# A graph network's first stage: statistics, keys, checks and attention vectors made ahead of the loop over node blocks

## The chip, the core and the metric

The kernel runs on one core of a Trainium2 chip. A core has TensorE (PE, matrix products, with its weight loads shown as PEld), VectorE (DVE), ScalarE (ACT), GpSimd (POOL) and SyncE (SP), which issues most DMA transfers. The engines run side by side, each through its own list of instructions in order, and wait for each other by semaphores. The metric is the device time of one execution in microseconds (us); lower is better.

## The reference

The reference takes 3125 nodes with 256 features and 100,000 directed edges, sorted by target, and computes four residual blocks one after the other:

```python
x = x + gat2(layernorm(x))        # two graph attention layers: 4 heads of 256, then 1 head of 256
x = x + experts8(layernorm(x))    # the two best of 8 experts, chosen for all nodes together
x = x + gcn3(layernorm(x))        # linear, then two graph convolutions, each with relu
x = x + experts8_per_node(layernorm(x))   # two of 8 experts per node
```

Of the attention layer, this is what the changed stage prepares:

```python
h    = (x @ W1).reshape(N, 4, 256)
al_s = einsum('nhc,hc->nh', h, a_src)     # source logit of each node and head
al_d = einsum('nhc,hc->nh', h, a_dst)     # target logit
e    = leaky_relu(al_s[src] + al_d[dst], 0.2)
out  = segment_sum(h[src] * softmax_over_incoming(e), dst)
```

## The kernel before, in words

The nodes are 25 blocks of 128, held in five groups of five blocks. The logits need no `h`: W1 times the attention vectors gives one matrix `u1` of 256 x 8, and the normalised features times `u1` give all eight logits of a node. Likewise `u2` serves the second layer from W2.

The function concerned is `FirstLayer.run` (line 2080 on). Its first part, in the pool named `before`, does the following.

- `bounds` (L1418 on) finds first and last target of each chunk of 256 edges. `load_edges` loads sources and targets.
- `norm_rows` (L1538 on) normalises a group in two halves: statistics on VectorE (L1544, L1545), then a root on ScalarE (L1548), reciprocal and product on VectorE (L1549, L1550), five normalisations on ScalarE (L1553) and a store of the rows into a DRAM table (L1555).
- `attention_vectors` (L1570) makes `u1` or `u2`: 16 VectorE instructions of 128x256, each a product with its sum.
- `count_starts` (L1452 on), `keys` (L1505 on), `edge_starts` (L1462 on) and `check` (L1479 on) are VectorE work on the edge lists: where each chunk writes, the keys by which edges are counted, and flags that say whether the fast way was allowed.
- The loop over 25 blocks turns each block on TensorE (L2127, two transposes into PSUM, two PSUM buffers), copies it to `xt` on ScalarE (L2131), stores five blocks at a time to DRAM (L2133) and multiplies it with `u1` into the logits `pl` (L2135). At every fourth block a `count_step` goes along: it makes one-hot matrices of a chunk of edges on VectorE (L1666, L1669), multiplies them on TensorE (L1683) and adds the counts to `acc` on ScalarE and VectorE (L1700, L1705). The one-hot matrices have three buffers.
- `sd` takes the logits out of PSUM (L2137). `first_terms` reduces them to their extremes, over the partitions on GpSimd (L1589), and after its first `yield` makes the terms of the attention weights (L1596 on). SP writes them to the DRAM table behind the rows (L1598), to `terms` (L1602) and to `loops` (L1612). Six count steps stand between the two halves.

After that the pool `before` is closed, and its room goes to the buffers of the main loop (`open_sums`). GpSimd begins to gather source rows from the table (L1790), one indirect DMA per 128 edges, eight to a batch, with room for three batches. SP loads turned blocks and the self-loops' weights, broadcast to all partitions (L1914, L1916), and for each chunk a window of target terms and the places of its edges (L1800, L1803). VectorE joins gathered terms with target terms (L1833) and spreads the weights over the one-hot matrices (L1844). TensorE sums the gathered rows by target (L1856), and VectorE adds the sums up (L1873). The main loop interleaves these edge steps with the count steps and with a dense part for the 256 lowest targets.

What sets the order: VectorE's instructions of the first part are tied to the written order (`k.in_order` with VectorE alone). TensorE, ScalarE, GpSimd and the queues of the first part are ordered by the framework's scheduler. In the main loop the written order holds for TensorE, VectorE and ScalarE. A tile takes the room of a closed pool only when all users of that room are done.

In the part that changes, the order of the source before is this:

```python
for g in range(GR + 1):            # statistics and normalisation of five groups
    ...
    if g == 2:
        self.attention_vectors("1", tmp, u1, ...)
self.count_starts(tmp); self.keys(tmp)
for b in range(NB): ...            # turn, copy, store, multiply; xt has two buffers
```

Of the kernel before, what the change touches and what calls it, by code (L numbers as in the profile page):

```python
# [11 lines left out]
F32 = mybir.dt.float32  # L12
# [12 lines left out]
P = 128  # L25
# [3 lines left out]
D = 256  # L29
# [1361 lines left out]
class FirstLayer:  # L1391
# [692 lines left out]
    def run(self, src_cols, dst_cols, dst_rows, x_in, keep, stats, u2):  # L2084

        tc, nc, k, I = self.tc, self.nc, self.k, self.I
        with ExitStack() as ctx:
            pool = ctx.enter_context(tc.tile_pool(name="edges", bufs=1))
            self.open_counts(ctx, pool)
            w1 = pool.tile([P, 2, 4 * D], F32, name="w1_all")  # L2090
            with tc.tile_pool(name="before", bufs=1) as tmp, \
                    tc.tile_pool(name="ps_in", bufs=1, space=PSUM) as psum, \
                    tc.tile_pool(name="ps_turn", bufs=2, space=PSUM) as turn:
                start = len(nc.cur_bb.bb.instructions)
                self.bounds(dst_rows, tmp)
                self.load_edges(src_cols, dst_cols, tmp)
                nc.gpsimd.dma_start(w1, I["L0_gnn_W1"].rearrange("(c p) f -> p c f", p=P))
                for b in range(0, NB, GB):
                    last_x = nc.sync.dma_start(
                        k.x[:, b:b + GB, :],  # L2100
                        x_in[b * P:(b + GB) * P, :].rearrange("(b p) f -> p b f", p=P))
                nc.vector.memset(k.rows[:, :, D:], 1.0)
                groups = [self.norm_rows(
                    k.x[:, b:b + GB, :],
                    self.table[b * P:(b + GB) * P, :D].rearrange("(b p) f -> p b f", p=P), tmp)
                    for b in range(0, NB, GB)]
                u1 = tmp.tile([P, 2, 8], F32, name="u1")
                for g in range(GR + 1):
                    if g < GR:
                        next(groups[g])  # L2110
                    if g == 2:
                        self.attention_vectors("1", tmp, u1,
                                               w1.rearrange("p c (k f) -> p k c f", k=4))
                    if g > 0:
                        next(groups[g - 1])
                self.count_starts(tmp)
                self.keys(tmp)
                pl = psum.tile([P, 512], F32, name="pl")
                sd = tmp.tile([P, NB, 8], F32, name="sd")
                i = 0  # L2120
                for b in range(NB):
                    if b % 4 == 0:
                        self.count_step(i)
                        i += 1
                    pt = turn.tile([P, 512], F32, name="turn")
                    for c in range(2):
                        nc.tensor.transpose(pt[:, ts(c, P)], k.x[:, b, ts(c, P)], k.ident)  # L2127
                    if b % GB == 0:
                        xt5 = tmp.tile([P, 2, GW], F32, name="xt", bufs=2)
                    xt = xt5[:, :, ts(b % GB, P)]  # L2130
                    nc.scalar.copy(xt, pt[:, :2 * P].rearrange("p (c n) -> p c n", c=2))  # L2131
                    if b % GB == GB - 1:
                        nc.sync.dma_start(self.turned[:, :, (b + 1) * P - GW:(b + 1) * P], xt5)  # L2133
                    for c in range(2):
                        nc.tensor.matmul(pl[:, 8 * b:8 * b + 8], lhsT=xt[:, c, :],  # L2135
                                         rhs=u1[:, c, :], start=(c == 0), stop=(c == 1))
                nc.vector.tensor_copy(sd.rearrange("p b k -> p (b k)"), pl[:, :8 * NB])  # L2137
                w2 = tmp.tile([P, 8, D], F32, name="w2")
                load = nc.gpsimd.dma_start(w2, I["L0_gnn_W2"].rearrange("(c p) f -> p c f", p=P))
                tc.add_manual_dep(load.ins, last_x.ins.name, SYNC)  # L2140
                parts = self.first_terms(sd, pool)
                next(parts)
                self.edge_starts(tmp)
                for _ in range(6):
                    self.count_step(i)
                    i += 1
                next(parts)
                self.attention_vectors("2", tmp, u2, w2.rearrange("p (k c) f -> p k c f", c=2))
                self.check(tmp)
                k.in_order({}, start, [mybir.EngineType.DVE])  # L2150
            self.open_sums(ctx, w1, stats)
            for c in range(RB * BC):
                self.fetch(c)
            for task in self.new_sums(0):
                task()
                self.count_step(i)
                i += 1
            self.tasks.extend(self.new_sums(1))
            for m in range(2):
                for c in range(self.size[m]):  # L2160
                    self.window(m, c)
            self.count_step(i)
            i += 1
            self.place_edges(0)
            self.pick_terms(0)
            self.count_step(i)
            i += 1
            self.place_edges(1)
            self.weigh_edges(0)
            self.spread_edges(0)  # L2170
            self.open_dense()
            e = s = 0
            i0, d0 = i, CUT[1] + 6
            engines, last = [mybir.EngineType.PE, mybir.EngineType.DVE, mybir.EngineType.Activation], {}
            start = len(nc.cur_bb.bb.instructions)

            d1 = d0 + 3
            while i < C1 + 3 or e <= NE or s < len(self.steps) or self.tasks or self.later:
                if i < C1 + 3:
                    self.count_step(i)  # L2180
                if i == d0:
                    self.lead(0)
                later, self.later = self.later, []
                if self.tasks:
                    self.tasks.popleft()()
                share = (FIRST * (i - i0) / (d1 - i0) if i < d1 else
                         FIRST + (NE + 1 - FIRST) * (i - d1) / (C1 - d1))
                while e <= NE and e <= share:
                    self.edge_step(e)
                    if e == NE:  # L2190
                        self.tasks.extend(self.through_w1(AS - 1))
                    e += 1
                while s < len(self.steps) and i > d0 + 3 and \
                        s * (C1 - 12 - d0) <= (i - d0 - 3) * len(self.steps):
                    self.dense_step(s)
                    s += 1
                for f in later:
                    f()
                start = k.in_order(last, start, engines)
                i += 1  # L2200
# [490 lines left out]
```

## Time and profile before

| | us |
|---|---|
| median of 4 runs | 2582.72 |
| the runs | 2575.94, 2579.74, 2585.70, 2598.34 |
| the profiled execution's own time | 2580.89 |
| its span | 2579.1 |
| TensorE busy | 2289.0 (89%) |
| VectorE busy | 1379.2 (53%) |
| ScalarE busy | 1152.6 (45%) |
| GpSimd busy | 828.6 (32%) |
| mean granted TensorE clock | 0.932 |
| first gather issued | 103.91 |

Busy time is the sum of an engine's instructions. In the rows of the timeline the columns are: start in us from the span's start, length in us, engine, line of the source, operation, what it writes and reads, and in brackets how long the engine had been idle and what ended that. A releaser in brackets is inferred from semaphores: where an instruction waits for several, it is the one that came last. An engine name with a q (SPq, POOLq) is that engine's sequencer, where DMA transfers are issued.

### The profile page before, as it was taken

The page shows a single profiled execution, that of the slowest core. Times are in us where ns is not written, and L with a number is a line of the kernel's source. Part 1 is how long each engine was busy: PE and PEld are TensorE (multiplying, and loading weights), DVE is VectorE, ACT ScalarE, POOL GpSimd, SP SyncE. Part 2 cuts the span into 40 slices and gives each one's busy share as a digit, 9 for nine tenths or more (in the row PEclk, how much of TensorE's full clock was granted, in tenths as well). Part 3 has the DMA queues.
Part 4 walks back from the last instruction along what each step waited for, and adds up shares of the span by engine and source line. Part 5 has one row for each costly group of instructions (what it writes and reads, how often), then busy time and mean ns, then how long its engine had stood idle before and what let it go on. Part 6 is the DMA issues. An engine that isn't in the chain of part 4 may idle for free. (4 is left out here: it accounts for less than half of the span.)

```text
span 2579.1 us, 38754 instructions
## 1 busy us (share of the span) xinstructions
PE 2289.0 (89%) x11821; PEld 1866.6 (72%) x11821; DVE 1379.2 (53%) x4362; ACT 1152.6 (45%) x2556; POOL 828.6 (32%) x803
## 2 busy tenths in 40 slices
PE   2489989998989987779999699979989989999996
PEld 2378777877767664668888588858867667888886
DVE  6677666677777874217888623433326663111110
ACT  2277655666656652504454334544434333222221
POOL 1365576777677870200010110000001213221211
PEclk9999877899899996899999899989999988999998
DMA  6543455566566662885222100023334435656662
GB/s 203 107 111 94 133 152 165 138 193 182 166 191 191 192 183 75 310 308 181 68 73 70 57 1 1 1 77 128 115 103 133 142 135 158 196 167 189 172 191 53
DMA packets 241725, 355.00 MB, mean 138 GB/s; under 512 B 45360, under 2 KB 182931, under 8 KB 237794
## 3 DMA queue, kind: packets, MB, share of 16 engines
q1 hardware_dynamic: 197762, 253.10, 31.0%
q0 software_dynamic: 40176, 94.81, 14.2%
q10 hardware_dynamic: 3568, 4.47, 0.6%
q8 instruction: 100, 1.64, 0.3%
q14 instruction: 119, 0.97, 0.1%
HBM read 266.60 MB, written 86.86 MB: 137 GB/s over the span
## 5 line engine op out<-in xcount | busy, mean ns | idle before, releaser
L1790 POOL DMA_INDIRECT edge_rows<-table,pick x566 | 605.0, 1069 | 236.0 <-PE edge_sums L1856 102.0
L1856 PEld LDWEIGHTS edge_sums<-edge_moves,edge_rows 128*128 128x128 f32 x2264 | 355.2, 232 | 49.4 <-DVE agg L1873 24.4
L1856 PE MATMUL edge_sums<-edge_moves,edge_rows 128*128 128x56 f32 (+1 forms) x2264 | 359.3, 313 | 17.4 <-DVE agg L1873 17.4
L1089 PE MATMUL po<-parts,cnt_r 128*128 128x512 f32 x1250 | 325.6, 413 | 14.1 <-ACT cnt_r L1083 14.1
L1089 PEld LDWEIGHTS po<-parts,cnt_r 128*128 128x128 f32 x1250 | 237.6, 195 | 74.1 <-ACT cnt_r L1083 14.9
L853 PE MATMUL po<-h,w 128*128 128x257 f32 x1250 | 279.0, 384 | 6.7 <-DVE w L844 4.4
L853 PEld LDWEIGHTS po<-h,w 128*128 128x128 f32 x1250 | 237.5, 192 | 43.6 <-DVE w L844 6.4
L1700 ACT CAST acc<-ps 128x325 f32 (+2 forms) x391 | 177.8, 455 | 196.6 <-DVE acc L1705 103.0
L1683 PE MATMUL ps<-hot_key,hot_lo 128*128 128x350 f16 (+2 forms) x782 | 216.4, 382 | 49.6 <-DVE acc L1705 25.5
L2567 ACT ACTIVATE hid<-ph,ffn_b 128x256 f32<-128x256 f32 x232 | 109.8, 473 | 298.7 <-PE ph L2565 298.7
L1666 DVE TENSOR_SCALAR hot_key<-iota_key,key 128x350 f16<-128x350 f16 (+2 forms) x782 | 233.4, 326 | 10.0 <-PE ps L1683 7.6
L2565 PE MATMUL ph<-xe,ffn_w 128*128 128x256 f32 x928 | 210.3, 382 | 3.1 <-DVE ng_mv L1015 3.1
L2575 PE MATMUL py<-ffn_w,hid 128*128 128x256 f32 x928 | 209.2, 383 | 0.0
L2579 POOL DMA_INDIRECT out<-y,to x58 | 90.4, 1559 | 347.0 <-DVE y L2578 251.3
L2565 PEld LDWEIGHTS ph<-xe,ffn_w 128*128 128x128 f32 x928 | 174.2, 191 | 30.1 <-DVE ng_mv L1015 3.3
L2575 PEld LDWEIGHTS py<-ffn_w,hid 128*128 128x128 f32 x928 | 176.3, 193 | 23.3
L838 ACT ACTIVATE z<-z,att_cols 128x640 f32<-128x640 f32 x125 | 103.0, 828 | 151.7 <-DVE z L836 128.8
L1672 ACT ACTIVATE hot_lo<-iota_key,lo 128x128 f16<-128x128 f16 x494 | 169.0, 391 | 0.0
L1083 ACT CAST cnt_r<-cnt_h 128x1920 fp32r<-128x1920 f16 x50 | 90.0, 1800 | 137.9 <-PE po L1089 130.0
L1683 PEld LDWEIGHTS <-hot_lo 128*128 128x128 f16 x782 | 68.3, 111 | 99.5 <-ACT hot_lo L1675 22.9
L2036 PE MATMUL po<-x_rows,w 128*128 128x257 f32 x400 | 130.7, 456 | 0.7 <-DVE w L2027 0.7
L2275 POOL IOTA earlier<- 128x128 f32 x1 | 0.2, 243 | 398.1 <-PE po L1089 398.1
(399 smaller groups left out, 3483.7 us busy)
## 6 DMA issues: line engine op xcount, KB each, us to landing
ffn_w<-in_L_ffn_W SPq DMA_DIRECT2D x58, 1024.0 KB
cnt_h<-cnt SPq DMA_DIRECT2D x50, 800.0 KB
rows<-blank SPq DMA_DIRECT2D x109, 258.0 KB
cnt<-acc SPq DMA_DIRECT2D x50, 400.0 KB
cnt<-cnt SPq DMA_DIRECT2D x25, 800.0 KB
normed<-first_out SPq DMA_DIRECT2D x20, 640.0 KB
first_out<-first SPq DMA_DIRECT2D x56, 192.0 KB
edge_rows<-table,pick POOLq DMA_INDIRECT x566
```

The costliest lines, as they stand in the source:

```text
L853: nc.tensor.matmul(pos[i][:, :D + 1], lhsT=w[:, ts(i, P)], rhs=moving[:, j, :D + 1], start=(j == 0), stop=(j == NB - 1))
L1089: nc.tensor.matmul(pos[b], lhsT=c[:, j - j0, ts(b, P)], rhs=parts[i][:, j].rearrange("p a m -> p (a m)"), start=(j == 0), stop=(j == NB - 1))
L1666: nc.vector.tensor_scalar(h[:, u, :NB * w], self.wide[:, :NB * w], self.key[:, t:t + 1], None, op0=ALU.is_equal)
L1672: nc.scalar.activation(l[:, u, :], self.wide[:, :P], AF.Abs, bias=self.lo[:, t:t + 1], scale=-1.0)
L1683: self.nc.tensor.matmul(ps[:, :n], lhsT=l[:, u, :], rhs=h[:, u, :n], start=(u == 0), stop=(u == CT - 1))
L1700: self.nc.scalar.copy(self.acc[g][:, :, ds(o + 1, width(c) - 1)], self.parts[c][:, :, 1:])
L1790: self.nc.gpsimd.indirect_dma_start(out=self.ring[:, e % (RB * BT), :], out_offset=None, in_=self.table, in_offset=bass.IndirectOffsetOnAx ...
L1856: nc.tensor.matmul(ps[:, f * 4 * w:(f + 1) * 4 * w], lhsT=self.rows_of(m)[:, e, ts(f, P)], rhs=self.moves[m][:, e].rearrange("p k w -> p ( ...
L2036: self.nc.tensor.matmul(self.pos[i][:, :D + 1], lhsT=w[:, ts(i, P)], rhs=self.k.rows[:, j, :], start=(j == 0), stop=(j == NB - 1))
L2565: nc.tensor.matmul(ph, lhsT=w1[:, c, ts(f, P)], rhs=xe[:, c, :], start=(c == 0), stop=(c == 1))
L2567: nc.scalar.activation(hid[:, f, :], ph, AF.Gelu, bias=b1[:, f:f + 1])
L2575: nc.tensor.matmul(py, lhsT=hid[:, f, ts(i, P)], rhs=w2[:, f, :], start=(f == 0), stop=(f == NF - 1))
```

## The change

Six things, all in `FirstLayer.run`:

- the making of `u1` no longer stands between the groups of the statistics, but behind all of them;
- `edge_starts` and `check` come ahead of the loop over blocks, behind `keys`; before, they stood behind the first half of `first_terms` and at the end;
- `u1` is made behind `check`, ahead of the loop;
- the load of W2 is written ahead of the loop;
- `u2` is made between the loop and the copy of the logits, where before it came behind the second half of `first_terms`;
- `xt` has five buffers of five blocks instead of two.

Nothing is computed differently.

```diff
                 for g in range(GR + 1):
                     if g < GR:
                         next(groups[g])
-                    if g == 2:
-                        self.attention_vectors("1", tmp, u1,
-                                               w1.rearrange("p c (k f) -> p k c f", k=4))
                     if g > 0:
                         next(groups[g - 1])
                 self.count_starts(tmp)
                 self.keys(tmp)
+                self.edge_starts(tmp)
+                self.check(tmp)
+                self.attention_vectors("1", tmp, u1, w1.rearrange("p c (k f) -> p k c f", k=4))
+                w2 = tmp.tile([P, 8, D], F32, name="w2")
+                load = nc.gpsimd.dma_start(w2, I["L0_gnn_W2"].rearrange("(c p) f -> p c f", p=P))
+                tc.add_manual_dep(load.ins, last_x.ins.name, SYNC)
                 pl = psum.tile([P, 512], F32, name="pl")
...
                     if b % GB == 0:
-                        xt5 = tmp.tile([P, 2, GW], F32, name="xt", bufs=2)
+                        xt5 = tmp.tile([P, 2, GW], F32, name="xt", bufs=GR)
...
+                self.attention_vectors("2", tmp, u2, w2.rearrange("p (k c) f -> p k c f", c=2))
                 nc.vector.tensor_copy(sd.rearrange("p b k -> p (b k)"), pl[:, :8 * NB])
-                w2 = tmp.tile([P, 8, D], F32, name="w2")
-                load = nc.gpsimd.dma_start(w2, I["L0_gnn_W2"].rearrange("(c p) f -> p c f", p=P))
-                tc.add_manual_dep(load.ins, last_x.ins.name, SYNC)
                 parts = self.first_terms(sd, pool)
                 next(parts)
-                self.edge_starts(tmp)
                 for _ in range(6):
                     self.count_step(i)
                     i += 1
                 next(parts)
-                self.attention_vectors("2", tmp, u2, w2.rearrange("p (k c) f -> p k c f", c=2))
-                self.check(tmp)
                 k.in_order({}, start, [mybir.EngineType.DVE])
```

## The prediction

> **What bounds the kernel now.** I read the page first: TensorE is busy 89% of the span, but its costliest groups lie behind the place of the change, which is in the first 103 us. So I then asked for busy time by stretch, and for the events at the end of that stage.
>
> ```profile
> span 2579.1 us, 38754 instructions
> ...
> PE 2289.0 (89%) x11821; PEld 1866.6 (72%) x11821; DVE 1379.2 (53%) x4362; ACT 1152.6 (45%) x2556; POOL 828.6 (32%) x803
> ...
> 81.00:85.00 4.00, 0.00 (x0) 0.10 (x1) 3.83 (x23) 0.00 (x0) 0.45 (x1) 1.00 0.42 161
> 85.00:90.00 5.00, 2.86 (x12) 1.07 (x11) 4.61 (x30) 2.09 (x6) 0.00 (x0) 1.00 0.00 0
> 90.00:103.00 13.00, 0.93 (x6) 0.55 (x5) 12.90 (x70) 2.01 (x5) 0.04 (x1) 1.00 1.16 15
> ...
> 121.00:130.00 9.00, 3.67 (x19) 2.99 (x19) 0.85 (x5) 0.05 (x1) 6.72 (x8) 1.00 0.75 222
> ```
>
> The columns of the stretches are: length, busy PE, PEld, DVE, ACT, POOL, granted clock, share of the DMA engines, GB/s. From 90 to 103 us only VectorE works (12.90 of 13.00 us): it prepares the terms, multiplies out W2's attention vectors (16 steps, 91.98 to 97.58) and runs the checks (97.51 to 102.58). From 121 to 130 VectorE stands still. The timeline and the waits say for what:
>
> ```profile
> 80.91 0.37 DVE L2137 COPY sd<-pl 128x200 f32<-128x200 f32 x1 [6.35 <-PE pl L2135]
> ...
> 89.41 0.27 DVE L1596 TENSOR_TENSOR s_terms<-sd,ends_all 128x100 f32<-128x100 f32 x1
> ...
> 100.89 1.76 DVE L1490 TENSOR_REDUCE doubt<-bad 1x1 f32<-1x1564 f32 x1
> ...
> 102.96 0.16 POOL L1767 IOTA place<- 128x20 f32 x1 [20.07 <-DVE window L1772]
> ...
> 103.91 1.19 POOL L1790 DMA_INDIRECT edge_rows<-table,pick  x1 [0.70 <-issue]
> ...
> 129.50 0.19 DVE L1833 TENSOR_TENSOR edge_p<-aux,edge_rows 128x32 f32<-128x32 f32 x1 [8.11 <-DMA edge_rows<-table,pick]
> ...
> POOL edge_rows L1790 <- PE edge_sums L1856: 46.7, 38, 4.0
> ```
>
> The checks' scratch lies in the pool that must close before the gather buffers open, so GpSimd waits for VectorE's last check and issues the first gather at 103.91. Sixteen gathers, about 1.25 us apart and some longer, bring the second batch at 129.50; VectorE waited 8.11 us for it. Between 165 and 300 us (last line) it is the gathers that wait for TensorE: the loop then runs at TensorE's pace. What counts is therefore **when the batch of 129.50 can start**; what moves it moves everything after it, one for one, up to the end.
>
> **The change, step by step.** VectorE's order in this stage is written out by hand, so I follow it.
>
> *Statistics.* W1's vectors (38.86 to 44.38, 5.5 us) leave this place. VectorE doesn't gain all of it: the last reciprocal needs the root of the fifth group, which ScalarE now issues behind the normalisations of four groups (2.57 us each). ScalarE: groups 0 and 1 to 41.8, two roots to 42.3, two copies to 43.0, group 2 to 45.6, a copy, group 3 to 48.5, root at 48.8. VectorE has its statistics at 45.5, waits 3.3 us, and goes on at 49.2 instead of 52.82: 3.6 us won.
>
> *What is moved ahead.* Starts and keys 9.0 us (52.82 to 61.82), edge starts 1.9 (82.23 to 84.13), checks 4.6 (5.07 less three interleaved count instructions), W1's vectors 5.5: the vectors are ready at 49.2 + 9.0 + 1.9 + 4.6 + 5.5 = 70.2, where before they were at 44.38.
>
> *Turned blocks.* With five tiles for them instead of two, TensorE's order is now 50 transposes, then the logit matmuls. Transposes with no matmul between them ran once: five copies began at 38.78 to 41.06, 0.57 us a block; with matmuls between a block took 1.17 (66.19 to 72.06). Nineteen blocks remain after the last normalisation (about 52.2): done at 63.0 by the first row, 74.4 by the second. I take 63.0, as the same work; they hide behind VectorE. At the other end 4 us come onto the path.
>
> *Logits.* Fifty 128x8 matmuls at 0.22 (20 in 4.43 us) are 11 us, formerly spread through the transposes, now in a row from 70.4; three count chunks (0.49 each) stand among them: done at 82.9. The fourth chunk, which TensorE has behind them, ends at 83.4; the seventh count step on VectorE needs its buffer, so VectorE is free at about 84.5. **Only then come W2's vectors, 5.5 us, ahead of the copy of the logits**: that copy falls at 90.0 instead of 80.91. Copy and reductions 1.3, six count steps 5.3 (84.13 to 89.41): the terms begin at 96.6 instead of 89.41, **7.2 us later**. The all-reduce on GpSimd (0.45) has 5.3 us of cover left of 7.1.
>
> *The end of the stage.* Behind the terms nothing remains: W2's vectors (5.5), checks (4.6) are gone, and the pool closes at once. Late next is the write of the terms into the table. It was issued at 90.00; its bytes flowed from 91.0 to 92.8 at 54 GB/s, and the trace's completion events end at 94.45. Moved by 7.2 that is 101.7, and a gather can start at about 102.0 against 103.91: **1.9 us won**. The gather needs no other late thing: the keys are earlier, and so are the tables of rows.
>
> *Three queues behind it.* SP issues the terms, then the small loop weights, whose 16-byte packets keep the DMA engines over-full (share 1.16) until 102.5; their landing, which SP waited for, came at 105.64. All of that moves by 7.2 to 112.8. From it hang the three broadcast loads, and behind these on SP the windows and edge places, which VectorE and TensorE need before the second batch. VectorE was ready for that batch at 121.4; plus 7.2 is 128.6, still ahead of 129.50, and in the new order count steps stand ahead of the wait for the broadcast, which makes it some 2 us better. So rows (129.50 - 1.9 = 127.6) and preparation (126.6 to 128.6) end nearly together. The first gathers now run while those 16-byte packets still flow; before, they started after them. No row shows that mix: nothing, if the 1.25 us issue pace hides it, up to 2.8 us, the longest stretch of one gather (2.77 against 0.95) amid broadcast loads. I take 0.5. GpSimd's W2 load and SP's row tables move past nothing that waits.
>
> Sum: -1.9 + 0.5 = **about -1.5 us**. Against the profiled execution's own 2580.89 (span 2579.1, 1.8 around it) that is 2579.4. That execution lies 1.8 below the median of the four runs, 2582.72 (2575.94 to 2598.34), so I say **2580**.
>
> One rule speaks against the change. The row: TensorE stood idle from 80.87 to 85.11, 4.2 us, and the next pair of count matmuls took 0.49 us, against 0.54 for the same form among others, at a granted clock of 1.00. The Trainium skill (TensorE: Matmul & The Clock Gate, Part 1: The HAM clock gate) says that an idle window of about 3.4 us sets the clock to half until a busy window has passed. The new idle time ahead of the logits is longer than that; by the rule the first 3.4 us of logit matmuls would do half their work, an estimate of 1.7 us more, and the sum would be about +0.2. By the row it costs nothing, and I go by the row.
>
> **Rivals.**
>
> *Slower: the late chain takes the wait's place.* W1's vectors at 70.2 instead of 44.4 and W2's vectors ahead of the logits make the terms later than 7.2. It decides from about 9 us of delay (101.7 + 1.9 would be the old gather start). If the transposes run at 1.17, the delay is 11.2: gathers at 106.0 (+2.1), preparation at 121.4 + 11.2 = 132.6 (+3.1): 2584. With the longest gather disturbance on top, +5.9: 2587. For it: VectorE is nearly the only engine at work there, and the change lengthens its run ahead of the logits by 25.8 us (70.2 - 44.4). Against: 10.1 us leave the end.
>
> *Faster: the count steps pack better.* The six steps hold about 0.6 us of gaps, and the mixed count and logit matmuls may overlap; 2 to 3 us off the 7.2 put the gathers at 99.5 and the preparation at about 125: -4, 2577.
>
> *Nothing arrives.* The order on VectorE and on the queues is the same from the first spread of edges on, so the loop repeats itself; but if TensorE's pace, not the second batch, sets the loop after 165 us, a change of 2 us may be taken up there (the gathers had 46.7 us of waits for TensorE between 165 and 300 us, so they run ahead). Then 0: 2581. That the room for blocks does nothing, since two PSUM buffers still pace the transposes, is part of this: price nil.
>
> *Far away:* the granted clock (mean 0.93, down to 0.71 between 364 and 464 us) could fall differently; no reason in the change.
>
> **How the numbers follow.** Forecast (-3 to 0) 0.45; slower rival (+1 to +8) 0.35; faster rival (-5 to -3) 0.08; nothing arrives 0.09; clock, either way, 0.03. The bounds of the cases, -5 to +8, give 2576 to 2589 about the profiled execution; runs of one kernel differ, from 5 below that execution to 17 above it, and a median of several by less, so I widen to 2573 to 2593. One per cent is 26 us, about what a measurement of this kernel can tell from no change: none of the mechanisms reaches it. Faster by over 1%: 0.02; within 1%: 0.95; slower by over 1%: 0.03.
>
> **What would show it.** Right: W1's vectors begin near 64.7 and end near 70.2; 50 transposes in a row before any logit matmul; the copy of the logits near 90; the terms near 96.6; no VectorE work between the terms and the buffers' clearing; first gather near 102; the second batch's VectorE instruction near 128, with a wait for gathers of a microsecond or less, or for broadcasts instead. Wrong, if the first gather falls later than 104, if VectorE waits for edge places or broadcasts past 130, or if anything after 200 us differs by more than the shift.

## The result: half a per cent slower

| | before | after |
|---|---|---|
| median, us | 2584.33 (63 runs) | 2597.10 (42 runs) |
| lowest and highest, us | 2559.85, 2604.89 | 2577.77, 2618.74 |
| the profiled execution's own time (span) | 2580.89 (2579.1) | 2588.80 (2587.0) |
| mean granted clock in it | 0.932 | 0.934 |

The ratio, taken over the fast executions (two of the changed kernel's, at 2618 and 2619 us, count as slow), is 1.0052, with a 95% interval of 1.0035 to 1.0069: 9.0 to 17.8 us of 2584. The forecast was 2580 with a range of 2573 to 2593; the kernel went the other way, and out of the range. It is the first rival, the late chain in the wait's place, that came, and more strongly than it was priced.

The page after shows the same number of instructions, and busy times that differ by less than 6 us on any engine. The time went into waits:

```profile
span 2587.0 us, 38754 instructions
...
PE 2287.4 (88%) x11821; PEld 1863.5 (72%) x11821; DVE 1380.1 (53%) x4362; ACT 1153.2 (45%) x2556; POOL 834.2 (32%) x803
```

Busy time by stretch after the change (length, busy PE, PEld, DVE, ACT, POOL, granted clock, DMA share, GB/s) shows a stage in which the engines take turns:

```profile
61.40:69.50 8.10, 0.04 (x1) 0.00 (x0) 8.07 (x36) 0.37 (x1) 0.00 (x0) 1.00 0.24 94
69.50:91.60 22.10, 22.05 (x110) 22.00 (x111) 5.27 (x30) 1.03 (x4) 0.00 (x0) 1.00 0.00 1
91.60:98.00 6.40, 1.11 (x6) 0.42 (x4) 6.40 (x38) 0.68 (x2) 0.00 (x0) 1.00 0.00 0
...
107.00:126.00 19.00, 3.77 (x15) 1.26 (x15) 6.68 (x38) 3.55 (x12) 10.85 (x13) 1.00 1.35 116
126.00:140.00 14.00, 4.64 (x24) 4.04 (x24) 10.38 (x23) 1.16 (x4) 11.67 (x8) 1.00 0.56 169
```

To 69.5 VectorE ends the checks and makes W1's vectors (from 64.2 on), and TensorE stands. Then TensorE works 22 us without a gap and VectorE is busy for 5 of them. Then VectorE makes W2's vectors and TensorE stands again. From 107 to 126 the DMA engines are over-full (1.35); GpSimd issues gathers, and the others have little to do. The timeline after the change gives the points of the chain:

```profile
69.55 4.43 PE L2138 MATMUL pl<-u,xt 128*128 128x8 f32 x20 [8.11 <-DVE att_scr L1570]
...
82.19 9.02 PE L2138 MATMUL pl<-u,xt 128*128 128x8 f32 x42
91.06 1.16 PE L1683 MATMUL ps<-hot_key,hot_lo 128*128 128x200 f16 x6
91.59 0.27 DVE L1666 TENSOR_SCALAR hot_key<-iota_key,key 128x200 f16<-128x200 f16 x1 [8.20 <-PE ps L1683]
97.92 0.36 DVE L2141 COPY sd<-pl 128x200 f32<-128x200 f32 x1
104.53 0.27 DVE L1596 TENSOR_TENSOR s_terms<-sd,ends_all 128x100 f32<-128x100 f32 x1
109.53 1.19 POOL L1790 DMA_INDIRECT edge_rows<-table,pick  x1 [2.45 <-DMA table<-s_terms]
121.77 1.30 SPq L1916 DMA_DIRECT2D by_node<-loops  x3
122.24 0.94 POOL L1790 DMA_INDIRECT edge_rows<-table,pick  x1 [2.66 <-DMA edge_rows<-table,pick]
125.99 3.88 DVE L1926 TENSOR_TENSOR agg<-loop_x,by_node 128x1024 f32<-128x1024 f32 x2 [11.39 <-DMA by_node<-loops]
139.13 0.19 DVE L1833 TENSOR_TENSOR edge_p<-aux,edge_rows 128x32 f32<-128x32 f32 x1 [2.38 <-DMA edge_rows<-table,pick]
```

Read it from the end. The second batch comes at 139.13; before, it came at 129.50: 9.6 us. VectorE was ready for it 2.38 us earlier, at 136.75, since the broadcasts (by_node) reached it late (11.39 us of waiting); these hang from the small writes, these from the terms at 104.53 (before 89.41: 15.1 us), these from the copy of the logits at 97.92 (before 80.91: 17.0 us). And the logits are 100 records in the trace, not 50: 42 of them took 9.02 us. The groups of the same stretch (count, then busy us and mean ns, then the idle time in front) say it in one line, and the view of before has the same count:

```profile
L2138 PE MATMUL pl<-u,xt 128*128 128x8 f32 x100 | 21.7, 356 | 8.1 <-DVE att_scr L1570 8.1
```

```profile
L2135 PE MATMUL pl<-u,xt 128*128 128x8 f32 x100 | 22.6, 344 | 7.5 <-ACT xt L2131 4.3 <-DVE att_scr L1570 3.2
```

The source has two matmuls a block, 50 in all; the trace has two records for each, in all kernels here, whereas the 50 transposes of the same type have one each. Behind the second batch the loop goes on as before: the ninth batch came at 234.3 instead of 224.1, the last at 982.2 instead of 972.8, and the span ended 7.9 us later. So in these two traces the shift of the first stage was carried through, as the prediction had it for any shift.

The changed kernel was slower elsewhere too. The experiments below ran on chips on which the kernel before took 2688 to 2692 us, so they are compared with it, and with the changed kernel, on chips of that pace. What one measurement there can tell is shown by the kernel before under another label (before_again, 12 runs against 35): 1.0027, interval 1.0001 to 1.0052. Differences under some 0.3% are therefore read from the events of the first 140 us, not from the medians. An event is read from one trace of each kernel: the second batch of the kernel before came at 129.50 and 131.44, that of the changed kernel at 139.13, 139.67 and 142.49, so of a difference in that column 2 to 3 us can be chance.

### The profile page after: what moved, and what is told of

Its sections match the earlier page's. It is cut to its first block, busy times and chain, and to the rows that moved or that the text cites. A ratio compares the mean times of both kernels' runs of the same rounds, so it can differ in the third digit from the quotient of the medians.

```text
span 2587.0 us, 38754 instructions
## 1 busy us (share of the span) xinstructions
PE 2287.4 (88%) x11821; PEld 1863.5 (72%) x11821; DVE 1380.1 (53%) x4362; ACT 1153.2 (45%) x2556; POOL 834.2 (32%) x803
## 3 DMA queue, kind: packets, MB, share of 16 engines
q0 software_dynamic: 40176, 94.81, 14.3%
## 5 line engine op out<-in xcount | busy, mean ns | idle before, releaser
L1089 PEld LDWEIGHTS po<-parts,cnt_r 128*128 128x128 f32 x1250 | 236.8, 194 | 74.1 <-ACT cnt_r L1083 14.8
```

What stands on the lines that cost most here:

```text
L1089: nc.tensor.matmul(pos[b], lhsT=c[:, j - j0, ts(b, P)], rhs=parts[i][:, j].rearrange("p a m -> p (a m)"), start=(j == 0), stop=(j == NB - 1))
```

## The experiments

The events in us; "ready" is the second batch's start less VectorE's wait just before it.

| kernel | copy of logits | terms | first gather | ready | second batch | ratio to before, interval |
|---|---|---|---|---|---|---|
| before_again | 80.73 | 89.24 | 103.74 | 124.2 | 131.44 | 1.0027 (1.0001, 1.0052) |
| after_again | 97.66 | 104.27 | 109.13 | 140.0 | 142.49 | 1.0045 (1.0022, 1.0068) |
| after_control | 98.12 | 104.74 | 109.62 | 137.1 | 139.67 | 1.0064 (1.0034, 1.0094) |
| vectors1_early | 87.26 | 93.89 | 98.82 | 129.2 | 133.28 | 0.9993 (0.9972, 1.0014) |
| vectors1_early_ordered | 87.62 | 94.24 | 99.14 | 127.7 | 130.71 | 0.9997 (0.9975, 1.0019) |
| vectors2_late | 92.65 | 99.25 | 108.63 | 134.5 | 135.83 | 1.0006 (0.9985, 1.0028) |
| half_logits | 89.04 | 95.65 | 100.55 | 130.5 | 132.84 | 1.0011 (0.9995, 1.0028) |
| loop_rows | 97.95 | 104.57 | 109.46 | 135.7 | 139.20 | 1.0009 (0.9985, 1.0032) |
| late_vectors1_before | 91.60 | 100.11 | 114.55 | 133.3 | 141.15 | 1.0023 (0.9998, 1.0048) |
| checks_only | 81.00 | 87.60 | 97.04 | 125.4 | 126.50 | 0.9988 (0.9961, 1.0015) |
| two_buffers | 98.20 | 104.83 | 109.69 | 138.0 | 141.78 | 1.0043 (1.0021, 1.0066) |
| terms_first_ordered | 86.10 | 88.21 | 95.56 | 125.9 | 125.94 | 0.9988 (0.9961, 1.0016) |
| counts_behind | 78.28 | 80.36 | 87.89 | 126.5 | 126.45 | 1.0009 (0.9982, 1.0037) |
| counts_behind_room | 78.54 | 80.62 | 87.75 | 117.9 | 117.94 | 0.9984 (0.9956, 1.0013) |
| checks_only_room | 80.86 | 87.48 | 96.92 | 123.5 | 124.61 | 0.9987 (0.9962, 1.0012) |
| gathers_held | 98.27 | 104.89 | 109.75 | 137.3 | 145.67 | 1.0067 (1.0038, 1.0096) |

On these chips single traces keep a shift less well than the first two did. Against before_again, after_control is 8.2 us late at the second batch and 8.2 at the last one, after_again 11.1 and 18.7, late_vectors1_before 9.7 and only 0.7. A shift at the second batch is therefore what an edit does to the first stage; whether the time follows is for the medians to say.

The theory: the logits can't start before W1's vectors, and then 100 passes (records of the logits) in a row stand ahead of the count matmuls, of W2's vectors and of the terms; the terms set the stage.

**W1's vectors back in their old place.** The rest of the change stays.

```diff
                         next(groups[g])
+                    if g == 2:
+                        self.attention_vectors("1", tmp, u1, ...)
...
                 self.check(tmp)
-                self.attention_vectors("1", tmp, u1, ...)
```

> The changed kernel, with W1's vectors back between the second and third group of the statistics; all else as changed (edge starts, checks and W2's load ahead, W2's vectors ahead of the copy of the logits, five buffers). Theory (the logits, 100 passes and 21.5 us, can't start before W1's vectors at 69.8, and this is what lies on the path): the logit matmuls spread through the transposes again, the copy of the logits falls near 83 instead of 97.9, the terms near 89.6 to 91 instead of 104.5, the first gather near 95 to 97 instead of 109.5; the small writes still meet the gathers (+4), so the second batch near 125 instead of 139; span 12 to 15 us below the changed kernel, 3 to 6 below the one before. Rival A (W2's vectors ahead of the copy, 5.5 us, are what costs): the copy stays some 5.5 us later than before, terms near 95, and the span is at most 6 us below the changed kernel, no better than before. Rival B (the meeting of small writes and gathers costs all of it): within 3 us of the changed kernel.

The copy fell at 87.26 and the terms at 93.89, 10.4 to 10.9 us earlier than in the two traces of the changed kernel on chips of this pace, and the time was that of the kernel before (0.9993), where both traces of the changed kernel belong to measurements above 1.004. So W1's vectors are the larger part, and rival B is out. Rival A has a part too: its terms, near 95, are close, and what is left against the 89.2 of before_again is 4.7 us, W2's vectors. The copy was expected at 83; a wait of 8.15 us on VectorE shows why it came later:

```profile
78.56 0.27 DVE L1666 TENSOR_SCALAR hot_key<-iota_key,key 128x200 f16<-128x200 f16 x1 [8.15 <-PE ps L1683]
87.26 0.37 DVE L2143 COPY sd<-pl 128x200 f32<-128x200 f32 x1
93.89 0.25 DVE L1596 TENSOR_TENSOR s_terms<-sd,ends_all 128x100 f32<-128x100 f32 x1
```

The count step waits for a count matmul that TensorE has behind the logits, and only then come W2's vectors. The batch came at 133.28, against the 125 expected. Behind the terms it took 39.4 us instead of 35 to 38: SP issued two loads of turned blocks ahead of the third small write.

**That order tied**, for these loads and the first edge places, with nothing else changed:

```diff
-        self.nc.sync.dma_start(x, self.turned[:, :, ts(b, P)])
+        late = self.nc.sync.dma_start(x, self.turned[:, :, ts(b, P)])
+        self.tc.add_manual_dep(late.ins, self.small.ins.name, ORDER)   # self.small: the third small write
```

> The changed kernel with W1's vectors back between the second and third group of the statistics, and with the loads of turned blocks and edge places tied behind the small writes in SP's order (untied, the scheduler put two loads ahead of the third write). Terms at 93.9 and first gather at 98.8, as without the tie. Theory (terms, then small writes, then broadcasts, then the products with them: some 32 us from the terms to the second batch, 36 to 37 with the gathers running among the small writes): second batch between 127 and 131, so within 3 us of the kernel before, and 8 to 11 us below the changed kernel. Rival (only the order on SP made the batch late, not the gathers among the small writes): second batch at 126, 3.5 us below the kernel before.

The broadcasts were issued 18.7 us behind the first small write instead of 20.7, and the batch came at 130.71, 36.5 us behind the terms. That is the theory's number, not the rival's 126.

**W2's vectors back at the end**, W1's left where the change has them.

```diff
-                self.attention_vectors("2", tmp, u2, ...)
                 nc.vector.tensor_copy(sd.rearrange("p b k -> p (b k)"), pl[:, :8 * NB])
...
                 next(parts)
+                self.attention_vectors("2", tmp, u2, ...)
```

> The changed kernel, with W2's vectors behind the second half of the terms, as before the change. Theory (logits behind W1's vectors): the copy of the logits at 92.4 instead of 97.9, terms at 99.0; W2's vectors then end near 107 and hold the pool, so that the first gather is at about 107.5 (2 us better); second batch near 135 to 137; span 2 to 4 us below the changed kernel, still 5 to 7 above the one before. Rival A (W2's vectors ahead of the copy are the cause): the span falls by 8 to 10 us, to that of the kernel before. Rival B (meeting of the small writes and the gathers): these meet less, since the gathers start 8.5 us behind the terms instead of 5; span 4 us below.

Copy 92.65, terms 99.25, gather 108.63, second batch 135.83: each within 1.2 us of the theory's numbers. The terms are 5.0 to 5.5 us earlier than in the changed kernel, so W2's vectors ahead of the copy were a part of the damage, the smaller one: the terms stay 10 us behind those of the kernel before. In its median (1.0006) this kernel was nearer to the kernel before than expected, within what such a measurement leaves open.

**Half the logits.**

```diff
-                    for c in range(2):
-                        nc.tensor.matmul(..., lhsT=xt[:, c, :], rhs=u1[:, c, :], start=(c == 0), stop=(c == 1))
+                    nc.tensor.matmul(..., lhsT=xt[:, 0, :], rhs=u1[:, 0, :], start=True, stop=True)
```

> The changed kernel, with only the first half of each node's features multiplied into the logits (one matmul a block instead of two; the other half is left out, so the weights are others). Theory (100 passes at 0.215 us in a row stand on the path): 50 passes less are 10.7 us, VectorE's wait for the count matmuls behind them (16.8 us in all) falls to about 6, the copy of the logits is at about 87, terms 94, first gather 99; span 8 to 11 us below the changed kernel. Rival A (W2's vectors): the same order, so the gain is small only if the wait for the count matmuls is not the logits' doing: 0 to 3 us. Rival B (small writes and gathers): both move together, so 0 to 3 us as well.

```profile
L2137 PE MATMUL pl<-u,xt 128*128 128x8 f32 x50 | 10.9, 356 | 8.1 <-DVE att_scr L1570 8.1
...
DVE hot_key L1666 <- PE ps L1683: 7.8, 2, 6.6
```

The program now has 25 matmuls for the logits; the trace has 50 records and 10.9 us instead of 100 and 21.7. VectorE's wait for the count matmuls is 7.8 us instead of 16.8, and the copy came 8.6 to 9.1 us earlier with the order on VectorE unchanged. Copy, terms and gather were each some 2 us later than expected. This measures the term of the prediction by itself. The second batch gained 6.8 to 9.7 us, where rivals A and B had at most 3, so by the events both fall.

**W1's vectors late, alone, in the kernel before.**

```diff
                         next(groups[g])
-                    if g == 2:
-                        self.attention_vectors("1", tmp, u1, ...)
...
                 self.keys(tmp)
+                self.attention_vectors("1", tmp, u1, ...)
```

> The kernel before, with one part of the change alone: W1's vectors behind the keys instead of between the groups of the statistics. Theory (logits wait for W1's vectors and then have 100 passes of 0.215 us ahead of them): vectors ready near 63.2, twelve blocks turned by then, the other thirteen follow at 1.17 us a block; last logit near 89 to 90, copy near 90, terms near 98.5, first gather at 112 to 113 behind the old tail, second batch 8 to 10 us behind that of the kernel before, span 6 to 12 us above it. Rival (the turning of blocks, not W1's vectors, sets the logits' end): copy at 81 to 83, span within 3 us.

Copy 91.60 instead of 80.73, terms 100.11, second batch 141.15: 9.7 us behind before_again, with none of the other edits. This one edit alone delays the batch as much as the whole change (8.2 and 11.1 us in the two traces here). The time was expected 6 to 12 us longer; the median is 3.7 us longer, and its interval (0.9998 to 1.0048) holds no change. The theory is shown here by the events, not by the time. Its waits after 60 us, all of them for work that now lies behind the vectors:

```profile
DVE acc L1705 <- ACT acc L1700: 10.0, 2, 8.6
DVE sd L2135 <- PE pl L2133: 6.1, 1, 6.1
DVE hot_key L1666 <- PE ps L1683: 6.1, 2, 4.0
```

**Edge starts and checks ahead, alone, in the kernel before.**

```diff
                 self.keys(tmp)
+                self.edge_starts(tmp)
+                self.check(tmp)
...
                 next(parts)
-                self.edge_starts(tmp)
...
-                self.check(tmp)
```

> The kernel before, with another part of the change alone: edge starts and checks behind the keys, ahead of the loop over blocks. Theory (VectorE stood idle 7 and 6 us inside that loop, so 6.5 us fit in): copy of the logits still near 81, terms 87.5, W2's vectors behind them, pool closed near 96, first gather 96.5; second batch 36 to 38 us behind the terms, at 123 to 126 (131.4 for the kernel before on a chip like the last one); span 4 to 7 us below the kernel before. Rival (the checks push the count steps and with them the copy): copy at 86 to 88, terms at 93, nothing won, span within 2 us.

Copy 81.00, terms 87.60, first gather 97.04, second batch 126.50. The idle time of VectorE inside the loop over blocks took the 6.5 us in: the two waits of 7.2 and 6.4 us of the kernel before are down to 3.14 and 3.64 here.

```profile
73.78 0.27 DVE L1666 TENSOR_SCALAR hot_key<-iota_key,key 128x200 f16<-128x200 f16 x1 [3.14 <-PE ps L1683]
78.99 0.26 DVE L1705 TENSOR_TENSOR acc<-acc,ps 128x25 f32 x1 [3.64 <-ACT acc L1700]
...
81.00 0.36 DVE L2139 COPY sd<-pl 128x200 f32<-128x200 f32 x1
...
87.60 0.26 DVE L1596 TENSOR_TENSOR s_terms<-sd,ends_all 128x100 f32<-128x100 f32 x1
```

This part of the change was good: 4.9 us at the second batch against before_again, 3.0 against the first trace of the kernel before. The median was 2.6 us lower, with an interval that holds no change.

**Two buffers for turned blocks in the changed kernel** (`bufs=2` for `bufs=GR`).

> The changed kernel with two buffers for turned blocks instead of five. Theory: twelve blocks are turned when W1's vectors come at 69.8, the other thirteen then go at 1.17 us a block; last logit near 96 instead of 91.1, copy near 102.5, terms near 109, second batch 4 to 6 us later than in the changed kernel; span 14 to 20 us above the kernel before. Rival (logits in a row cost the same as logits among transposes, the room is worth nothing): copy near 98, span as in the changed kernel, 9 to 14 above the kernel before.

The copy came at 98.20, as in the changed kernel: the rival's number. But not for its reason. The logits did end later, near 98 instead of 91; but W2's vectors, which in the changed kernel start behind the logits, here ran beside them (91.90 to 97.5), and the copy then waited 0.70 us for the last of them. So the room brought nothing as it was used, and W2's vectors could have been hidden, had the count step not stood ahead of them.

**The terms earlier still.** Checks inside the loop over blocks, and five of six count steps behind the terms.

```diff
                 next(parts)
-                for _ in range(6):
-                    self.count_step(i)
-                    i += 1
+                self.count_step(i)
+                i += 1
                 next(parts)
+                for _ in range(5):
+                    self.count_step(i)
+                    i += 1
```

> As the one before it, and besides: edge starts and checks inside the loop over blocks, ahead of the fourth count step, where VectorE stood idle for 7 us; one count step instead of six between the two halves of the terms, five behind them. Theory (the terms' time sets the stage): copy of the logits at 81 to 83, terms at 84 to 86 instead of 89.4 before and 104.5 after; first gather 5 us behind them; second batch 36 to 37 us behind them, at 120 to 123; span 6 to 9 us below the kernel before and 15 to 19 below the changed one. Rival (the gathers' start sets the stage): first gather 14 us earlier than before, so second batch at 115 to 117 and span 12 to 14 below the kernel before. Rival (the loop over blocks is held by the checks in it): terms later than 89.

Terms 88.21, later than expected, since VectorE stood 6.33 us until 78.57 for ScalarE's `acc`, which ScalarE has behind its copies of blocks; the gather came 7.4 us behind the terms instead of 5, as GpSimd waited for a count matmul until 95.13. The batch came 37.7 us behind the terms, at 125.94 and not at 120 to 123. The length is near the theory's 36 to 37; the first gather was 8.2 us earlier than in before_again and the batch 5.5, so the gathers' start alone did not set it.

**All count steps behind the terms**, none in the loop over blocks (one step between the halves, twelve behind).

> The changed kernel with W1's vectors back between the groups of the statistics, the loads tied behind the small writes on SP, no count step in the loop over blocks, one between the two halves of the terms and twelve behind them. Theory (the terms set the stage, and VectorE has 13 us of idle behind them in which the count steps fit): copy of the logits at 79 to 80, terms at 81 to 82, first gather at 87 to 89, second batch 36 to 38 us behind the terms, at 117 to 120; span 8 to 14 us below the kernel before. Rival (VectorE becomes the bound behind the terms): second batch at 122 to 126, span 3 to 8 below. Rival (what is won ahead of 130 us is lost in the loop): second batch at 117 to 120, span within 3 us of the kernel before.

Copy 78.28 and terms 80.36, a little ahead of what was expected, gather 87.89 as expected; but the batch came at 126.45. Neither rival: VectorE was not full, it waited for a transfer.

```profile
103.77 1.97 DVE L1930 TENSOR_TENSOR agg<-loop_x,by_node 128x1024 f32<-128x1024 f32 x1 [5.53 <-DMA by_node<-loops]
106.45 1.97 DVE L1930 TENSOR_TENSOR agg<-loop_x,by_node 128x1024 f32<-128x1024 f32 x1
116.19 1.97 DVE L1930 TENSOR_TENSOR agg<-loop_x,by_node 128x1024 f32<-128x1024 f32 x1 [6.84 <-DMA loop_x<-x_turned]
```

The third turned block needs a buffer that the first product frees; its load stood on SP behind windows and edge places, and was issued at 113.14.

**A third buffer for that load** (`name="loop_x", bufs=3`), in this kernel and in checks_only.

> The kernel with the count steps behind the terms, with three buffers instead of two for the turned blocks that the self-loops load, so that the third load needn't wait for the first product. Terms at 80.4, first gather at 88 as before it. Theory (the late third load was what kept VectorE): no wait of 6.8 us, second batch at 118 to 121 instead of 126.5; span 8 to 14 us below the kernel before. Rival (SP's list of sixteen windows and edge places, 0.9 us each, sets it): second batch 122 to 125, span 4 to 8 below. Rival (what is won early is lost in the loop): span within 3 us of the kernel before.

> The kernel before with edge starts and checks behind the keys and, besides, three buffers instead of two for the turned blocks that the self-loops load. Terms at 87.6, first gather at 97. Theory (as above, with the terms 7 us later): second batch at 123 to 125 instead of 126.5, span 5 to 9 us below the kernel before. Rival (windows and edge places on SP set it): no change from 126.5, span 3 to 6 below.

The batches came at 117.94 and 124.61, 8.5 and 1.9 us earlier than without the buffer: the theory's numbers, though the second difference is no larger than that between two traces of one kernel. Against the changed kernel beside them (1.0064) both are faster, by 19.6 and 22.0 us of median; against the kernel before, the medians are 8.0 and 10.4 us lower, and the intervals end at 1.0013 and 1.0012. So they beat the changed kernel, and that they beat the kernel before is likely from the traces but not shown by the times.

**Small packets against gathers.** First, one of the small writes in longer pieces:

```diff
-        nc.sync.dma_start(self.loops.rearrange("(b p) k -> p b k", p=P), own)
+        nc.sync.dma_start(self.loops.rearrange("(p b) k -> p b k", p=P), t[:, DB:, :])
```

> The changed kernel, with the small write of the self-loops' weights as 368 contiguous bytes a partition instead of 23 pieces of 16 bytes (taken from the target terms, and in another order: the weights of the self-loops become others). Terms stay at 104.5 and the first gather at 109.5. Theory (of the 9.6 us by which the second batch is late, 5.6 come from the terms and 4 from the small packets that run among the first gathers): the sixteen gathers take 25.6 us again instead of 29.6, VectorE's wait of 11.4 us for the broadcast falls to 2 to 4, the second batch is near 135, the span 3 to 5 us below the changed kernel. Rival A (the terms alone): no change in the span, within 1.5 us. Rival B (the meeting is all of it): 8 to 10 us below.

The broadcasts were issued 14.6 us behind the first write, where the changed kernel took 16.6 to 19.6, and the ninth gather waited 0.44 us for another to land instead of 2.66 to 6.15. But the batch came at 139.20, no earlier than in after_control: the gathers were then stretched beside the broadcasts, which now came earlier (2.74, 1.58 and 3.57 us for three of them). No gain at the batch, against the 3 to 5 expected in the span. The median (1.0009) is lower than such a batch would have it; why stays open. Then the other way round, the gathers held back until the third write had landed:

```diff
             first = self.nc.gpsimd.indirect_dma_start(...)
+            if e == 0:
+                self.tc.add_manual_dep(first.ins, self.small.ins.name, SYNC)
```

> The changed kernel, with one wait more: the first gather waits for the landing of the self-loops' small write, so that no gather runs among the small packets. Terms stay at 104.5. Theory (each holds the other: writes some 1 to 2 us longer, gathers 4 us longer when they meet): the broadcasts are issued 15.6 to 17.3 us behind the terms' write, as in the kernel before, instead of 16.6 to 19.6; sixteen gathers take 25.6 to 27.7 us again; but they start 12 us later, at about 121, so the second batch falls at 147 to 149 and the span is 5 to 9 us above the changed kernel. Rival (only the gathers suffer): broadcasts no earlier than in the changed kernel, the rest the same. Rival (the meeting costs nothing): gathers still take 30 us and more, second batch past 151.

```profile
112.56 0.95 POOL L1790 DMA_INDIRECT edge_rows<-table,pick  x1 [0.30 <-issue]
122.55 0.95 POOL L1790 DMA_INDIRECT edge_rows<-table,pick  x1 [9.04 <-DMA loops<-own_w]
```

The scheduler put three other gathers ahead of the held one, so thirteen were held. The broadcasts were issued 16.4 us behind the first write, in after_control 16.7: the gathers hardly hold the writes here. But 16.4 also lies in the theory's range (15.6 to 17.3), so this run does not tell the theory from the rival "only the gathers suffer". The batch came at 145.67, ahead of the 147 to 149 expected. Thirteen gathers from 122.55 to the batch took 23.1 us, though no small packet was left, since among them three were stretched (2.69, 1.58, 3.56) as the broadcasts flowed. Sixteen gathers took 29.6, 30.1 and 33.4 us in the three traces of the changed kernel, 25.6 and 27.7 in the two of the kernel before. So the meeting with small packets costs some 2 to 8 us, and holding the gathers back cost the batch more still: it came 6.0 us later than in after_control and 3.2 later than in after_again.

**The unchanged kernels on these chips:**

> The kernel before, unchanged, for its trace on the same chip as the three kernels beside it: terms at 89.4, first gather at 103.9, second batch at 129.5, time within 3 us of the runs of before around it.

> The changed kernel, unchanged, on the same chip: terms at 104.5, first gather at 109.5, second batch near 139, span 8 to 17 us above the kernel before, if the shift of the first 140 us is carried through the loop on any chip. Rival (a chip that grants TensorE less clock takes the shift up later): 0 to 6 us above.

> The changed kernel once more, beside the three others on the same chip: terms at 104.4, second batch 139 to 143, span 9 to 16 us above the kernel before.

The changed kernel was slower by 0.45% and 0.64%; beside the 0.45% the unchanged kernel before_again read 0.27%, so the second figure, on another chip, is the firmer one. The rival, that a chip with less clock takes the shift up (0 to 6 us), has both medians against it: 15.7 and 11.5 us.

## Why the prediction was wrong

**What held.** VectorE's list was followed rightly up to the logits: statistics done at 48.6 (49.2 forecast), W1's vectors ready at 69.8 (70.2), the last transposes at 61.4 (63.0; the first of the two rows was the right one), no VectorE work between terms and clearing, GpSimd waiting for the terms' write at last. The later links were right in length: terms to ready 32.2 us (before 32.0), and the batch's shift was kept to the end within 2 us.

**The step that failed: "Fifty 128x8 matmuls at 0.22 (20 in 4.43 us) are 11 us".** The count came from the source and the price from the trace, and the two don't fit: the 20 in the row are records, and a logit matmul leaves two. The logits measured 21.7 us, and ended at 91 instead of 82.9. That is an error of 10.7 us, and most of it stands in every number behind: the copy is late by 7.9 (97.92 against 90.0), the terms by 7.9 (104.53 against 96.6), the first gather by 7.5. With 21.7 in its place the same working gives terms some 18 us late; measured were 15.1. The rest was won back mainly in two places: the logits began at 69.55 and not at 70.4, and the three count chunks among them, priced at 1.5, took no time of their own (from 69.55 to 91.2 it is 21.7 us, the logits' own time). The row was at hand: a group by line and form says x100.

**The second term, the rest of the batch.** Of the 9.6 us, 7.25 come from VectorE being ready at 136.75 instead of being early for 129.50, and 2.38 from gathers that are later still. "Some 2 us better", for count steps ahead of the wait, did not come. The gathers among the small writes took 29.6 us instead of 25.6, so 4.0 and not the 0.5 chosen, above the bound of 2.8: a wait of the ninth gather for the landing of an earlier one (2.66 us) had no row before. Only 2.38 of it counts, since VectorE was late as well.

**The rival that came.** Its place and form were right, and "it decides from about 9 us of delay" fits the runs: with terms some 5 us late (vectors1_early and its ordered twin) the batch stayed within 2 us of before_again, with terms 10 us late (vectors2_late) it came 4.4 us later. Its sizes were built on transposes at 1.17 us, which did not happen, and the logits, which did it, were in nobody's price. Its bound of +8 lies below the measured interval, 9.0 to 17.8. And the one per cent that the forecast held for what a measurement can tell was too much: the interval is 8.8 us wide, and a change of half a per cent is clear.

**What the parts are worth, by the runs.** W1's vectors late, alone: 10.9 us at the terms, 9.7 at the second batch. W2's vectors ahead of the copy: 5.0 to 5.5 at the terms, 3.8 to 6.7 at the batch. Edge starts and checks ahead, alone: 1.6 us gained at the terms, 4.9 at the batch. Room for blocks: nothing. The parts add up: 14.3 to 14.8 us at the terms, where the changed kernel is 15.0 and 15.5 behind before_again, and 8.6 to 11.5 at the batch, where it is 8.2 and 11.1 behind.

**The clock rule.** The forecast weighed an estimate of 1.7 us from the Trainium skill (TensorE: Matmul & The Clock Gate, Part 1: The HAM clock gate) and chose nothing. In the profiled execution TensorE was idle 8.11 us and the granted clock stayed at 1.00. In three others the record fell to half in the idle time, as the rule says, but it did not come back when TensorE was busy again, and the time did not follow it; that is told at the end.

## What to carry to other kernels

Take count and price of a term from the same row: instructions in the source and records in the trace need not be the same number, and a group by line and form shows both. Before work is moved ahead "because it can be done early", ask which engine waits for the result of what it is moved in front of: here 6.5 us of checks fitted into VectorE's idle time for nothing, while moving the vectors that feed TensorE took 25 blocks' logits out of the shade of the transposes. And when a tail is taken away, look at the second chain beside it: here the small writes, the broadcasts and the products with them took 31 to 38 us from the terms to a ready VectorE in every kernel but one (46 in counts_behind, where a load came late), whenever the gathers started.

## What the runs showed of the hardware

**A clock in the record without an effect.** In after_again, after_control and gathers_held the granted clock falls to 0.50 between 61 and 66 us, within TensorE's idle time of 9 us, and the record stays there to 300 us at least. In the profiled execution of the result it stayed at 1.00 over 8.11 us of idle, and in two_buffers over 15.74. Busy time by stretch of after_control, and then of before_again:

```profile
70.00:90.00 20.00, 20.00 (x101) 20.00 (x101) 4.95 (x29) 1.03 (x3) 0.00 (x0) 0.50 0.01 1
160.00:300.00 140.00, 128.43 (x709) 105.24 (x710) 95.13 (x456) 98.28 (x313) 78.49 (x79) 0.50 0.36 97
```

```profile
160.00:300.00 140.00, 126.33 (x708) 102.99 (x707) 95.51 (x453) 96.72 (x304) 75.13 (x75) 1.00 0.37 99
```

From 160 to 300 us one executes 709 matmuls at a recorded 0.50, the other 708 at 1.00. Records of one form last as long at either: the 100 logit records take 356 ns at 0.50 (after_control) and at 1.00 (the result's trace), and the count matmuls of 128x350 in this stretch 493 ns at 0.50 (after_control) and at 1.00 (loop_rows). The times of the first measurement say the same: 7 of the 42 executions of the changed kernel have a mean clock of 0.88 to 0.89, and their median is 2596.0 us, that of the other 35 (0.92 to 0.94) 2597.4. A granted clock in the record is not yet a slower matmul, and the mean clock of 0.87 in these traces has this stretch in it.

**Few bytes, long writes.** The three small writes, 196 KB in all, in pieces of 32 and 16 bytes, kept the DMA engines at a share of 0.8 to 2.0 from 91 to 101 us in the kernel before, and their landing took longer still: the broadcasts that depend on the third were issued 15.6 and 17.3 us behind the first in the two traces of the kernel before, where all but the last two or three microseconds of it had no gather beside them, and 14.6 with that one write in pieces of 368 bytes and gathers beside it.

**SP stands too.** Two loads of turned blocks behind the small writes kept SP for 7.1 to 9.0 us in the three traces of the changed kernel (7.19 us from 109.28 on in the first). With the third write in pieces of 368 bytes (loop_rows) the same two took 1.25 us. That SP waits for room in its queue would fit, but isn't shown.

**Places differ.** The kernel before took 2584 us in the first measurement and 2688 to 2692 on the chips of the experiments. Its trace there has a granted clock of 0.72 between 300 and 500 us, where the first has 0.82; but the thirteenth batch is already 15 us later by then (302.4 against 287.3), at a clock of 1.00. What that is was not looked into.
